# A two-layer convolution block: two ky additions and the last batch norm on VectorE in the tail, a smaller kernel table, and two moves in the first group norm

## The chip, the cores and the metric

The kernel runs on one NeuronCore of one Trainium2 chip (trn2), in fp32. The metric is device microseconds of one execution. The engines are TensorE (PE, with its weight loads PEld), VectorE (DVE), ScalarE (ACT), GpSimd (POOL) and the queue engine SyncE (SP). DMAs are issued from the queues of SP, ScalarE and GpSimd.

## The reference

The input x is 32 images of 128 channels and 32x32 points. Two layers follow each other, each with a residual.

```python
# layer 0: h = group norm (32 groups) of x, as 1024 points of 128 channels
h = einsum('bdl,de->ble', u, W_enc) + b_enc            # 1024 channels
dtA = A * exp(log_dt)[:, None]; Bd = (exp(dtA) - 1) / A
K = 2 * einsum('dn,dnl->dl', Cc * Bd, exp(dtA[:, :, None] * t)).real   # t = 0..63, n = 0..3
y = gelu(causal_convolution(h, K) + D * h)
g = y @ W_glu + b_glu;  g = g[..., :1024] * sigmoid(g[..., 1024:])
x = x + layernorm(h + g) @ W_dec + b_dec
# layer 1: group norm, then a deformable depthwise 8x8 convolution:
# every one of 64 taps samples the image bilinearly at its own offset
acc = sum over taps of w_tap * bilinear(x, position + tap + offset)
x = x + gelu((acc - bn_mean) * bn_inv + bn_beta)
```

## The kernel before

**Table.** `ssm_kernel_table` computes K for all 1024 channels: 8 groups of 128 partitions with 4 terms n, so tiles of 128 partitions by 32 (channel group, n) pairs, and with the 64 steps t tiles of 128x2048. `sincos` reduces an angle (lines 68 to 73), takes two sines on ScalarE and squares the half-angle one. The result `kp` is stored to `kp_d` (line 159). The pool of the table is released afterwards, and the memory is used again by the tiles `z` of the next stage.

**Convolution stage.** `ssm_convolution` runs over 8 blocks k of 128 channels: `encode(k)` makes z, `convolve(k)` multiplies it with Toeplitz tables `toe` read from `kp_d`. Blocks 1 to 7 load u from `u_d`. Block 0 computes u, the group-normed image, on the way, in a loop over t that holds three images at different steps; every engine works through its queue in exactly the written order (`manual_schedule`). `group_norm_steps` yields five steps: the sum (ScalarE, line 169), a matmul (172), the negative mean and the square (ScalarE, 174 and 175), a matmul (178), and root, reciprocal and u (180 to 182). In the loop, image t-2 takes its last step and its u is stored to `u_d` (line 267); image t-1 takes the mean and the square; image t is loaded (272) and takes the sum; `image(t - 3)` multiplies the image that is three back with W_enc (line 237, eight matmuls in two groups g, fp32 matmuls appearing as two instructions each) and adds the bias into z (line 242); then the two matmuls of group norm for t-1 and t follow. u has five buffers, x six.

**Main block.** `main_block` runs two streams of work side by side, each a generator that yields estimated costs; `run_along` always advances the one whose progress is behind. The first stream, `first_parts`, is GLU, layer norm and decode (lines 815 to 875) of images 1 to 31. The second, `second_parts`, is the deformable convolution of all images: per image 17 packs of columns. For a pack, `ds` (hat weights in x, DMA line 1118) is multiplied by `dhy` (hat weights in y, DMA line 1133, shaped on ScalarE at 1153 and 1154) on VectorE at line 1159, TensorE multiplies the windows `dxw` with it (line 1235), and VectorE scales the result by the tap weights into `prod` (line 1251). `prod` has a section for every one of the eight ky. GpSimd adds the eight sections in seven additions, each in two halves (line 1278, 14 instructions), and adds the sum to `dacc` (1286). `prod` has two buffers, `ds` two, `dhy` three half-packs. On SP, the load of `dhy` for a later pack is written behind the multiply that frees its buffer, and the load of `ds` behind that. After an image GpSimd applies the batch norm (line 1297), ScalarE the gelu (1301), VectorE adds x (1302), and ScalarE's queue stores the result (1303). A second stream's step list (`prepare`) puts group norm, offsets (947), the relayout of offsets by DMA (991, 1006), the hat tables (1017 to 1019) and windows (1053) of the next image between the packs.

The first stream ends before the second; the remaining packs of the second run without it.

Of the kernel before, what the change touches and what calls it, by code (L numbers as in the profile page):

```python
# [8 lines left out]
F32 = mybir.dt.float32  # L9
AF = mybir.ActivationFunctionType  # L10
ALU = mybir.AluOpType
# [4 lines left out]
P = 128  # L16
B, C, H, W = 32, 128, 32, 32
# [4 lines left out]
NT = 64  # L22
# [19 lines left out]
def ssm_kernel_table(nc, tc, ins, kp_d):  # L42

    KN = KD * N2
    with tc.tile_pool(name="ssm", bufs=1) as sp:
# [6 lines left out]
        def small(tag, shape=(P, KN)):  # L52
            return sp.tile(list(shape), F32, tag=tag, name=tag)
# [7 lines left out]
        tt = sp.tile([P, NT], F32, tag="tt", name="tt")  # L61
        nc.sync.dma_start(tt, ins["steps"].to_broadcast([P, NT]))

        def sincos(theta, shape, tag):

            k = small(f"{tag}_k", shape)
            r = small(f"{tag}_r", shape)
            nc.vector.tensor_scalar(k, theta, INV_2PI, MAGIC, op0=ALU.mult, op1=ALU.add)
            nc.vector.tensor_scalar(k, k, MAGIC, None, op0=ALU.subtract)
            nc.vector.scalar_tensor_tensor(r, k, -PI2_A, theta, op0=ALU.mult, op1=ALU.add)  # L70
            nc.vector.scalar_tensor_tensor(r, k, -PI2_B, r, op0=ALU.mult, op1=ALU.add)
            nc.vector.scalar_tensor_tensor(r, k, -PI2_C, r, op0=ALU.mult, op1=ALU.add)
            nc.vector.tensor_scalar(r, r, PI_MAX, -PI_MAX, op0=ALU.min, op1=ALU.max)
            s = small(f"{tag}_s", shape)
            nc.scalar.activation(s, r, AF.Sin)
            nc.scalar.activation(k, r, AF.Sin, scale=0.5)
            nc.vector.scalar_tensor_tensor(r, k, -2.0, k, op0=ALU.mult, op1=ALU.mult)
            return s, r
# [45 lines left out]
        cbr, cbi = small("cbr"), small("cbi")  # L124
# [7 lines left out]
        nc.vector.tensor_scalar_mul(cbi, cbi, 2.0)  # L132


        big = (P, KN, NT)
        e, ang = small("e", big), small("ang", big)
        t_b = tt[:, None, :].to_broadcast([P, KN, NT])

        def over_t(a):
            return a[:, :, None].to_broadcast([P, KN, NT])  # L140

        nc.vector.tensor_mul(e, over_t(re), t_b)
        nc.scalar.activation(e, e, AF.Exp)
        nc.vector.tensor_mul(ang, over_t(im), t_b)
        sv, cv = sincos(ang, big, "v")
        nc.vector.scalar_tensor_tensor(cv, cv, 1.0, over_t(cbr), op0=ALU.add, op1=ALU.mult)
        nc.vector.tensor_mul(sv, sv, over_t(cbi))
        nc.vector.tensor_sub(cv, cv, sv)
        nc.vector.tensor_mul(cv, cv, e)

        kp = sp.tile([P, KD, KPW], F32, tag="kp", name="kp")
        nc.gpsimd.memset(kp, 0.0)
# [33 lines left out]
def ssm_convolution(nc, tc, const, ins, x, u_d, kp_d, y_d):  # L186
# [12 lines left out]
    with tc.tile_pool(name="cvt", bufs=3) as tp, tc.tile_pool(  # L199
        name="cvz", bufs=1  # L200
    ) as zp, tc.tile_pool(name="cv1", bufs=1) as one, tc.tile_pool(
        name="cvu", bufs=5
    ) as up, tc.tile_pool(name="cvy", bufs=6) as yp, tc.tile_pool(
        name="cvg", bufs=4
    ) as gp, tc.tile_pool(name="cv_ps", bufs=4, space=PSUM) as psum:

        def banks(name):
            return psum.tile([P, 2, 512], F32, tag="ps", name=name)
# [11 lines left out]
        def block(g, j):  # L220

            return 2 * ORDER[j] + g

        def encode(k):

            z = [
                pool.tile([P, P // 2, NB, B, 2], F32, tag=f"z{g}", name=f"z_{k}_{g}")
                for g, pool in enumerate((one, zp))
            ]
            bias = b_enc[:, k * P : (k + 1) * P]  # L230

            def image(b, u):
                both = banks(f"psz_{k}_{b}").rearrange("p g (j d) -> p g j d", j=NB)
                for g in range(2):
                    for j in range(NB):
                        lo = block(g, j) * P
                        nc.tensor.matmul(  # L237
                            both[:, g, j, :], u[:, lo : lo + P], w_enc[:, k * P : (k + 1) * P],
                            start=True, stop=True,
                        )  # L240
                for g in range(2):
                    nc.vector.tensor_add(  # L242
                        z[g][:, :, :, b, :].rearrange("p d j e -> p j d e"),
                        both[:, g].rearrange("p j (d e) -> p j d e", e=2),
                        bias.rearrange("p (d e) -> p d e", e=2)[:, None].to_broadcast(
                            [P, NB, P // 2, 2]
                        ),
                    )

            if k > 0:  # L250
                for b in range(B):
                    u = up.tile([P, L], F32, tag="u", name=f"u_{k}_{b}")
                    nc.sync.dma_start(u, u_d[b])
                    image(b, u)
                return z


            running = {}

            def step(b):  # L260
                if b in running:
                    next(running[b][1])

            for t in range(B + 3):
                step(t - 2)
                if t - 2 in running:
                    nc.scalar.dma_start(u_d[t - 2], running[t - 2][0])
                step(t - 1)
                if t < B:
                    u = up.tile([P, L], F32, tag="u", name=f"u_{k}_{t}")  # L270
                    xt = yp.tile([P, L], F32, tag="yo", name=f"xt_{t}")
                    nc.sync.dma_start(xt, x[t])

                    def pm(n, t=t):
                        return banks(f"gn_ps_{t}_{n}")[:, 0, 0:1]

                    running[t] = u, group_norm_steps(
                        nc, gp, pm, const["gavg"], const["eps"], xt, u
                    )
                    step(t)  # L280
                if t >= 3:
                    image(t - 3, running.pop(t - 3)[0])
                step(t - 1)
                step(t)
            return z

# [82 lines left out]
        with tc.manual_schedule():  # L369
            for k in range(KD):  # L370
                convolve(k, encode(k))
# [218 lines left out]
def main_block(nc, tc, const, ins, x, u_d, y_d, x1_d, out, offmax):  # L590
# [22 lines left out]
    with ctx:  # L613
# [78 lines left out]
        for i in range(2):  # L692
            t = dram1.tile([2, NCOL], F32, tag=f"rel_d{i}", name=f"rel_d{i}")
            rel_d.append(t)
            t = dram1.tile([P, 2 * ASTEP // P], F32, tag=f"rel_n{i}", name=f"rel_n{i}")
            n = 2 * ASTEP // P
            for lo in range(0, n, HSUB):
                w = min(HSUB, n - lo)
# [381 lines left out]
        packs = [(b, us) for b in range(B) for _, us in PACKS]  # L1080
# [98 lines left out]
        def second_part(b, steps):  # L1179
# [6 lines left out]
            for n in range(NP):  # L1186
# [6 lines left out]
                h = b * NP + n  # L1193
                s = s_of.pop(h)

                for i in range(0, PIECES, 2):
# [10 lines left out]
                    for piece in (i, i + 1):  # L1207
# [7 lines left out]
                        for parts in zip(blocks_of(0, piece), blocks_of(1, piece)):  # L1215
                            rows, run = parts[0][0][1], parts[0][0][3]
                            hi = lo + rows * run * m
                            to = [
                                t[:, lo:hi].rearrange("p (s k v) -> p s k v", s=m, k=rows)
                                for t in ps  # L1220
                            ]
                            for part in range(len(parts[0][1])):
                                for side in range(2):
                                    (ky, _, v0, _, step, skew), wins = parts[side]
                                    w, r0, r1 = wins[part]
                                    half = slice(64 * side, 64 * side + 64)
                                    frm = s[half, 0, ky * NV + v0 - VBASE[side] + r0 :]
                                    frm = bass.AP(
                                        tensor=frm.tensor, offset=frm.offset,
                                        ap=[  # L1230
                                            frm.ap[0], [CELLS, m],
                                            [step * NV + skew, rows], [1, r1 - r0],
                                        ],
                                    )
# [38 lines left out]
                def row(ky, lo=0, hi=m):  # L1273
                    return prod[:, ky * KS + lo * H : ky * KS + hi * H]

                for to, frm in ((2, 0), (3, 1), (4, 6), (5, 7), (2, 4), (3, 5), (2, 3)):
                    for lo, hi in ((0, m // 2), (m // 2, m)):
                        nc.gpsimd.tensor_add(  # L1278
                            row(to, lo, hi), row(to, lo, hi), row(frm, lo, hi)
                        )  # L1280
                total = row(2)
                slot = 0
                for u in us:
                    j0, nj = span_of(u)
                    to = acc[:, u - 7 + j0 : u - 7 + j0 + nj]
# [8 lines left out]
            o = two.tile([P, L], F32, tag="img", name=f"do_{b}")  # L1294
            xr = two.tile([P, L], F32, tag="img", name=f"dxr_{b}")
            nc.sync.dma_start(xr, x1_d[b])
            nc.gpsimd.tensor_scalar(
                o.rearrange("p (h w) -> p w h", w=W), acc, bn_mean, bn_inv,
                op0=ALU.subtract, op1=ALU.mult,
            )  # L1300
# [1 line left out]
            ending.append((11, lambda: nc.vector.tensor_add(o, o, xr)))  # L1302
            ending.append((14, lambda: nc.scalar.dma_start(out[b], o)))

        ending = []
        def measure(slots):

            return slots * 8.0 + 40.0
# [22 lines left out]
        def first_parts():  # L1331

            for b in range(1, B):
                for cost in first_part(b, last=(b == B - 1)):
                    yield cost / FIRST

        def second_parts():

            for cost in opening():
                yield AHEAD * cost / 82.0  # L1340
            for b in range(B):
                steps = prepare(b + 1) if b + 1 < B else []
                for cost in second_part(b, steps):
                    yield cost / SECOND

        run_along((first_parts(), 1.0), (second_parts(), 1.0))
        for _, step in ending:
            step()
# [145 lines left out]
```

## Time and profile before

| | |
|---|---|
| time, median of 3 | 12572.89 us (12570.41 to 12574.23) |
| the profiled execution | 12590.62 us, of it 12588.9 span |
| mean granted TensorE clock | 0.979 |
| PE busy | 12115.7 us (96%) |
| DVE busy | 7661.0 us (61%) |
| ACT busy | 5537.8 us (44%) |
| POOL busy | 8789.7 us (70%) |
| first `psy` matmul of the convolution of block 0 | 181.25 us |
| last matmul of the GLU stream (gpv) | 12116.5 us |
| last batch norm on GpSimd | 12572.49 to 12577.13 us |

Times inside the profile are counted from the start of the span. A row of the timeline gives start and duration, engine, line and operation, output and inputs, shape and count; in brackets stands the idle time of the engine before it and what ended it. A row of the table of waits gives who waited for whom, the total in us, how often, and the longest. The chain of waits is followed back from the last instruction to whatever released it at each step.

### The profile page before, as it was taken

What the parts mean: (1) busy time and instruction counts of PE and PEld (TensorE: products, weight loads), DVE (VectorE), ACT (ScalarE), POOL (GpSimd) and SP (SyncE); (2) the same over time, 40 slices, a digit from 0 to 9 for tenths busy, and PEclk for the clock granted to TensorE, in tenths of its full rate; (3) what the DMA queues carried; (4) which work ended last, traced back from release to release, by engine and by line L of the source; (5) the groups of instructions that cost most, each with busy time, mean ns of one, the idle gap of its engine ahead of it and who ended that gap; (6) DMA issues with size and microseconds to landing.
All of it is one profiled execution on the core that took longest, in us unless ns stands there. A gap on an engine that the chain in (4) does not pass through costs nothing.

```text
span 12588.9 us, 161534 instructions
## 1 busy us (share of the span) xinstructions
PE 12115.7 (96%) x51362; PEld 6608.0 (52%) x51362; DVE 7661.0 (61%) x14315; ACT 5537.8 (44%) x7852; POOL 8789.7 (70%) x11691
## 2 busy tenths in 40 slices
PE   7999889999999999999999999999999999999975
PEld 7999444444444444444444444444444444444443
DVE  5555136666666666666666666666666666666666
ACT  4344124444444444444444444444444444444444
POOL 2455227777777777777777777777777777777778
PEclk9999999999999999999999999999999999999986
DMA  7899236766666666666666666666667667666666
GB/s 236 267 276 277 83 98 185 187 184 184 180 183 180 185 178 182 186 184 181 188 184 187 184 180 185 179 187 180 179 187 186 180 186 186 186 185 184 183 176 177
DMA packets 1521947, 2350.43 MB, mean 187 GB/s; under 512 B 619586, under 2 KB 835266, under 8 KB 1520066
## 3 DMA queue, kind: packets, MB, share of 16 engines
q1 hardware_dynamic: 1382210, 2027.97, 60.1%
q10 hardware_dynamic: 89728, 177.76, 4.2%
q0 software_dynamic: 49152, 134.28, 3.6%
q8 instruction: 414, 6.78, 0.2%
q14 instruction: 443, 3.63, 0.1%
HBM read 2016.61 MB, written 407.02 MB: 193 GB/s over the span
## 4 chain that ended last, share of the span: by engine, by line
PE 77%; DMA 10%; ACT 5%; DVE 3%; issue 2%; SPq 2%; POOL 1%; ACTq 0%; DVEq 0%; POOLq 0%
PE gpv L838 24%; PE gpg L815 23%; PE dps L1235 15%; DMA dhat<-dh 5%; PE psy L320 5%; PE psz L237 3%; PE gpo L743 3%; PE gph L854 3%; DMA rel_d<-rel_n 1%; ACT dh L1018 1%; ACT dh L1017 1%; ACT dhy L1153 1%; POOL prod L1278 1%; DVE ds L1159 1%; DMA dr<-rel_d 1%
## 5 line engine op out<-in xcount | busy, mean ns | idle before, releaser
L1278 POOL TENSOR_TENSOR prod<-prod 128x256 f32<-128x256 f32 (+3 forms) x7616 | 5531.4, 767 | 1211.5 <-DVE prod L1251 1211.5
L1251 DVE TENSOR_TENSOR prod<-dps,k_weight_slots 128x512 f32<-128x512 f32 (+16 forms) x8704 | 3127.5, 407 | 1948.0 <-PE dps L1235 1743.5
L815 PE MATMUL gpg<-gy,g_w_glu 128*128 128x512 f32 x8192 | 3741.9, 600 | 14.3 <-DMA gy<-y_d 14.3
L838 PE MATMUL gpv<-gy,g_w_glu 128*128 128x512 f32 x8192 | 3732.1, 599 | 0.0
L1235 PE MATMUL dps<-ds,dxw 64*128 64x128 f32 (+14 forms) x23936 | 2700.2, 371 | 235.4 <-DVE prod L1251 171.5
L1159 DVE TENSOR_TENSOR ds<-ds,dhy 128x640 f32<-128x640 f32 (+2 forms) x2176 | 2260.0, 1075 | 929.0 <-ACT dhy L1154 673.3
L1235 PEld LDWEIGHTS dps<-ds,dxw 64*128 64x128 f32 x23936 | 1924.2, 194 | 1287.3 <-issue 480.6
L815 PEld LDWEIGHTS gpg<-gy,g_w_glu 128*128 128x128 f32 x8192 | 1511.2, 190 | 1926.2 <-issue 1862.1
L838 PEld LDWEIGHTS gpv<-gy,g_w_glu 128*128 128x128 f32 x8192 | 1514.6, 190 | 1909.2 <-issue 1909.2
L739 POOL TENSOR_TENSOR gs<-gs,gq 128x256 f32<-128x256 f32 x896 | 865.7, 987 | 1820.8 <-ACT gq L875 1820.8
L1153 ACT ACTIVATE dhy<-dhy,k_minus_y 128x640 f32<-128x640 f32 (+2 forms) x2176 | 1697.8, 780 | 384.2 <-DMA dhy<-rel_d 138.1
L1154 ACT ACTIVATE dhy<-dhy,one 128x640 f32<-128x640 f32 (+2 forms) x2176 | 1725.8, 793 | 71.2
L875 ACT ACTIVATE gq<-gr 128x512 f32<-128x512 f32 x448 | 282.3, 630 | 2793.1 <-DVE gr L867 2775.9
L822 ACT ACTIVATE gs<-gpg,k_b_glu 128x512 f32<-128x512 f32 x512 | 350.8, 685 | 1657.0 <-PE gpg L815 1655.7
L357 POOL DMA_DIRECT2D y_d<-yo x1024 | 591.5, 585 | 692.2 <-ACT yo L344 634.1
L846 DVE SCALAR_TENSOR_TENSOR gs<-gpv,k_b_glu,gs 128x512 f32<-128x512 f32 x512 | 382.9, 748 | 1008.6 <-PE gpv L838 983.2
L1286 POOL TENSOR_TENSOR dacc<-dacc,prod 128x256 f32<-128x256 f32 (+6 forms) x1184 | 862.8, 729 | 55.2
L739 POOL TENSOR_TENSOR gs<-gs,gr 128x256 f32<-128x256 f32 x896 | 798.0, 911 | 0.0
L320 PE MATMUL psy<-toe,z 128*128 128x192 f32 x4096 | 668.3, 326 | 7.6 <-DVE z L242 5.5
L320 PEld LDWEIGHTS psy<-toe,z 128*128 128x128 f32 x4096 | 663.4, 196 | 11.7 <-DVE z L242 6.8
L854 PE MATMUL gph<-gu,k_W_enc 128*128 128x512 f32 x1024 | 529.2, 598 | 27.7 <-DVE gs L846 27.4
L335 DVE TENSOR_TENSOR psy<-psy,t 128x256 f32<-128x256 f32 (+2 forms) x768 | 333.8, 435 | 346.3 <-ACT t L328 329.5
(164 smaller groups left out, 6020.0 us busy)
## 6 DMA issues: line engine op xcount, KB each, us to landing
dhy<-rel_d SPq DMA_DIRECT2D x3264, 160.0 KB
ds<-dhat SPq DMA_DIRECT2D x832, 400.0 KB
ds<-dhat SPq DMA_DIRECT2D x448, 480.0 KB
dxw<-dxw_d SPq DMA_DIRECT2D x832, 224.0 KB
y_d<-yo POOLq DMA_DIRECT2D x1024, 128.0 KB, 4.2
gy<-y_d SPq DMA_DIRECT2D x512, 256.0 KB
u<-u_d SPq DMA_DIRECT2D x224, 512.0 KB
dhat<-dh ACTq DMA_DIRECT2D x256, 390.0 KB
```

The source lines that it names most:

```text
L320: nc.tensor.matmul(ps[:, c // 2, c % 2, :], rows[i][:, (g * CG + c0 + c) // 2, c % 2, :], toe[:, c0 + c, :], start=True, stop=True,)
L739: nc.gpsimd.tensor_add(to[:, cut], to[:, cut], more[:, cut])
L815: nc.tensor.matmul(gate, w_glu[:, k, D + m * P : D + m * P + P], ys[k], start=(k == 0), stop=(k == KD - 1),)
L838: nc.tensor.matmul(val, w_glu[:, k, m * P : m * P + P], ys[k], start=(k == 0), stop=(k == KD - 1),)
L854: nc.tensor.matmul(h, w_enc[:, m * P : (m + 1) * P], u, start=True, stop=True)
L1153: nc.scalar.activation(t, t, AF.Abs, bias=minus_y)
L1154: nc.scalar.activation(t, t, AF.Relu, scale=-1.0, bias=const["one"])
L1159: nc.vector.tensor_mul(s_of[h][:, cut], s_of[h][:, cut], t)
L1235: nc.tensor.matmul(to[side][:, :, :, r0:r1], xw[half, w, :], frm, start=True, stop=True,)
L1251: nc.vector.tensor_mul(bass.AP(tensor=at_y.tensor, offset=at_y.offset, ap=[at_y.ap[0], [H, m], [step * (KS - 1) + skew, rows], [1, run],], ...
L1278: nc.gpsimd.tensor_add(row(to, lo, hi), row(to, lo, hi), row(frm, lo, hi))
L1286: nc.gpsimd.tensor_add(to, to, total[:, slot * H : (slot + nj) * H].rearrange("p (s y) -> p s y", y=H),)
```

## The change

It has four parts. The kernel table evaluates exponentials, sines and cosines only at 16 of the steps: the eight multiples (written 8a + 7 in the reversed order of the steps) and the last eight, and forms the 64 by complex products of the two, so that most tiles have 128x512 elements. In block 0, the store of u is issued from GpSimd's queue instead of ScalarE's, and the second group norm matmul of image t-1 stands between the two halves of the matmuls of image t-3 instead of behind them. In the packs that come after the first stream has ended, VectorE makes the additions of ky 0 into 2 and 1 into 3, each as one instruction, and in the very last pack those of 6 into 4 and 7 into 5 as well. The batch norm of the last image runs on VectorE.

```diff
-        big = (P, KN, NT)
-        e, ang = small("e", big), small("ang", big)
+        few = (P, KN, 16)
+        t16 = sp.tile([P, 16], F32, tag="t16", name="t16")
+        nc.vector.tensor_copy(t16[:, 0:8], tt[:, 7::8])
+        nc.vector.tensor_copy(t16[:, 8:16], tt[:, NT - 8 : NT])
+        e, ang = small("e", few), small("ang", few)
...
-        nc.vector.scalar_tensor_tensor(cv, cv, 1.0, over_t(cbr), op0=ALU.add, op1=ALU.mult)
-        nc.vector.tensor_mul(sv, sv, over_t(cbi))
-        nc.vector.tensor_sub(cv, cv, sv)
-        nc.vector.tensor_mul(cv, cv, e)
+        nc.vector.scalar_tensor_tensor(cv, cv, 1.0, e, op0=ALU.add, op1=ALU.mult)
+        nc.vector.tensor_mul(sv, sv, e)
+        w = [small(f"w{i}", (P, KN, 8)) for i in range(3)]
+        near = cv[:, :, 8:], sv[:, :, 8:]
+        nc.vector.tensor_mul(w[0], near[0], over_t(cbr, 8))
+        nc.vector.tensor_mul(w[2], near[1], over_t(cbi, 8))
+        nc.vector.tensor_sub(w[0], w[0], w[2])
+        nc.vector.tensor_mul(w[1], near[0], over_t(cbi, 8))
+        nc.vector.tensor_mul(w[2], near[1], over_t(cbr, 8))
+        nc.vector.tensor_add(w[1], w[1], w[2])
+        parts = []
+        for i, far in enumerate((cv, sv)):
+            o = small(f"o{i}", (P, KN, 8, 8))
+            nc.vector.tensor_mul(
+                o,
+                w[i][:, :, None, :].to_broadcast([P, KN, 8, 8]),
+                far[:, :, :8, None].to_broadcast([P, KN, 8, 8]),
+            )
+            parts.append(o.rearrange("p n a b -> p n (a b)"))
+        cv = parts[0]
+        nc.vector.tensor_sub(cv, cv, parts[1])
...
-            def image(b, u):
+            def image(b, u, between=None):
...
+                    if g == 0 and between is not None:
+                        between()
...
-                    nc.scalar.dma_start(u_d[t - 2], running[t - 2][0])
+                    nc.gpsimd.dma_start(u_d[t - 2], running[t - 2][0])
...
                 if t >= 3:
-                    image(t - 3, running.pop(t - 3)[0])
-                step(t - 1)
+                    image(t - 3, running.pop(t - 3)[0], between=lambda: step(t - 1))
+                else:
+                    step(t - 1)
...
                 for to, frm in ((2, 0), (3, 1), (4, 6), (5, 7), (2, 4), (3, 5), (2, 3)):
+                    if alone and frm in ((0, 1, 6, 7) if h + 1 == len(packs) else (0, 1)):
+                        nc.vector.tensor_add(row(to), row(to), row(frm))
+                        continue
...
-            nc.gpsimd.tensor_scalar(
+            finish = nc.vector if b == B - 1 else nc.gpsimd
+            finish.tensor_scalar(
...
-        ending = []
+        ending, alone = [], []
...
+            alone.append(True)   # at the end of first_parts
```

More of the change, by code (lines that the diff above doesn't have):

```diff
@@ L132, in ssm_kernel_table, with over_t @@
         nc.vector.tensor_scalar_mul(cbi, cbi, 2.0)
-        big = (P, KN, NT)
-        e, ang = small("e", big), small("ang", big)
-        t_b = tt[:, None, :].to_broadcast([P, KN, NT])
-        def over_t(a):
-            return a[:, :, None].to_broadcast([P, KN, NT])
+        few = (P, KN, 16)
[3 more added lines that the diff above has]
+        e, ang = small("e", few), small("ang", few)
+        t_b = t16[:, None, :].to_broadcast([P, KN, 16])
+        def over_t(a, n=16):
+            return a[:, :, None].to_broadcast([P, KN, n])
         nc.vector.tensor_mul(e, over_t(re), t_b)
@@ L144, in ssm_kernel_table @@
         nc.vector.tensor_mul(ang, over_t(im), t_b)
-        sv, cv = sincos(ang, big, "v")
-        nc.vector.scalar_tensor_tensor(cv, cv, 1.0, over_t(cbr), op0=ALU.add, op1=ALU.mult)
-        nc.vector.tensor_mul(sv, sv, over_t(cbi))
-        nc.vector.tensor_sub(cv, cv, sv)
-        nc.vector.tensor_mul(cv, cv, e)
+        sv, cv = sincos(ang, few, "v")
+        nc.vector.scalar_tensor_tensor(cv, cv, 1.0, e, op0=ALU.add, op1=ALU.mult)
[19 more added lines that the diff above has]
+        nc.vector.tensor_sub(cv, cv, parts[1])
         kp = sp.tile([P, KD, KPW], F32, tag="kp", name="kp")
```

## The prediction

> **What bounds the kernel now.** I read the slices of the page first. TensorE is 96% busy, and at full clock from about 200 us to 12130 us; the change touches nothing that runs there. What is left is two ends: the first 180 us (table, and group norm with encode of block 0) and the last 450 us, where the GLU matmuls have run out.
>
> ```profile
> PE   7999889999999999999999999999999999999975
> PEclk9999999999999999999999999999999999999986
> ```
>
> *The start: the timeline, then the table of waits for 50 to 185 us.* Columns: start, duration, engine, line, operation, and in brackets the idle time before it and what ended it.
>
> ```profile
> 42.05 0.39 SPq L159 DMA_DIRECT2D kp_d<-kp  x1
> 47.25 0.69 DVE L242 TENSOR_TENSOR z<-psz,b_enc 128x512 f32<-128x512 f32 x1 [5.27 <-DMA kp_d<-kp]
> ...
> 61.55 0.81 DVE L182 TENSOR_SCALAR u<-xt,gn_m,gn_r 128x1024 f32<-128x1024 f32 x1
> 62.40 0.34 ACTq L267 DMA_DIRECT2D u_d<-u  x1
> 62.79 0.17 ACT L174 ACTIVATE gn_m<-gn_ps 128x1 f32<-128x1 f32 x1 [1.47 <-DVE u L182]
> ```
> ```profile
> DVE z L242 <- PE psz L237: 47.7, 24, 3.1
> ACT gn_m L174 <- DVE u L182: 34.4, 22, 2.3
> ```
>
> To see: VectorE is held by the table until 42 us; the add into z then waits for the table's store, which still holds z's memory. After that every image has ScalarE stand still because the store of u, issued from its queue, waits for VectorE's u; gn_m of the next image is behind it. From the u at 48.05 to that of image 31 at 177.5 there are 29 steps, 4.46 us each (mostly 4.1, every third 5.3).
>
> *Why some take 5.3: the one-microsecond windows* (PE, PEld, DVE, ACT, POOL busy, granted clock, DMA share, GB/s).
>
> ```profile
> 107.00:108.00 1.00, 0.00 (x0) 0.00 (x0) 1.00 (x2) 0.70 (x2) 0.00 (x0) 1.00 0.28 74
> 109.00:110.00 1.00, 0.34 (x4) 0.26 (x3) 0.07 (x1) 0.90 (x3) 0.00 (x0) 1.00 1.00 377
> 112.00:113.00 1.00, 0.83 (x5) 0.54 (x3) 0.27 (x1) 1.00 (x3) 0.00 (x0) 0.50 0.97 209
> ```
>
> Clock 0.50 comes back for about 6.8 us of every 13.5 us, after some 3.5 us in which TensorE was about half busy. The 16 matmuls of an image then take 3.75 instead of 2.03 us.
>
> *The end: the chain of waits* (start, duration, what).
>
> ```profile
> 12498.43 8.91 DMA ds<-dhat
> 12507.43 0.06 DVE ds L1159
> ...
> 12512.90 12.01 POOL prod L1278 x14
> ...
> 12526.42 11.44 POOL prod L1278 x14
> ...
> 12539.34 11.57 POOL prod L1278 x14
> ...
> 12572.49 4.65 POOL do L1297
> 12577.16 1.16 ACT do L1301
> ```
> ```profile
> SPq L1133 <- DVE ds L1159: 73.3, 20, 10.0
> ```
>
> To see: from 12346 to 12509 a loop of loads sets the pace, some 14 us a pack: last weight multiply (L1159), SP issues dhy (L1133, which waits for it), then ds, the transfer of some 8 us, next multiply. GpSimd only binds from 12512.9 on, five packs, and in short pieces at 12137-12179 and 12328-12346.
>
> **The change part by part.**
>
> *Table.* Before, VectorE has ten two-input operations at 128x2048 (e, ang, three reductions of the angle, the square of the half angle, four combinations) at 2.29 us, and three TENSOR_SCALARs at 1.22: 26.5 us. After: e, ang, three reductions, square, cv and sv are 8 at 128x512 (0.69, rows L155-157) = 5.5; three TENSOR_SCALARs, between 0.17 (128x32) and 1.22, by line 0.42 each = 1.3; two copies 0.3; six products at 128x256, between 0.19 and 0.69, 0.42 each = 2.5; two 128x2048 products and the difference 6.9. Sum 16.5, so 10.0 less. ScalarE's three 1.9 us functions become about 0.63 (row L875). VectorE had hardly a gap here; shorter work shows waits for ScalarE's sines behind the image's own operations and table loads. I keep 8 of the 10 (ends: 5 and 11). The kp_d store (5.1) and the z add behind it move with it.
>
> *Store of u from GpSimd's queue.* 32 issues of 0.35 leave ScalarE, 32 of 0.585 (row L357, the same kind of store) go to GpSimd, which is 0.00 busy from 48 to 180; behind them in its queue are only the y stores from 191.9. The wait for u goes with the issue. What is late next: gn_m needs the mean's matmul (L172). Let T be the end of that matmul. ScalarE: gn_m to the square's end 1.50, to the identity's end 2.54. TensorE, with the square's matmul (L178) put between the two halves of the image: first half T to T+1.0, L178 waits to T+1.53, second half from T+1.77 to 2.79, L172 ends at T+3.17. So 3.2 us a step at full clock. This new wait of L178 holds the second half, L172 and the z adds; without it the step would be 2.95, so `between` by itself costs 0.2 here and gives an earlier root for the next u. VectorE (0.15 + 0.81 + 1.29) and the 16 DMA engines (share 0.64 x 4.46 = 2.9 a step) lie below. With DMA this near I take 3.5: 29 x (4.46 - 3.5) = 27.8 us. At half clock TensorE alone needs about 4.7.
>
> Here a rule is weighed. The row: the clock fell at 111 us after 3.5 us of half-busy TensorE with no gap over 2.2 us. The Trainium skill, "TensorE: Matmul & The Clock Gate" (What's actually happening), has it fall only after an idle window of about 3.4 us. By the rule the step would stay warm: 27.8. If, against it, windows as full as the new ones (2.8 of 3.5 us) still let it fall half of the time, the mean step is 13.5 / (6.75/4.7 + 6.75/3.5) = 4.0 and the gain 13. The trace contradicts the rule's letter, but the windows before a fall were 47-50% busy and the new ones would be 80%: I take warm.
>
> *Additions to VectorE.* The flag is set when the first stream is used up. By the yielded costs (31.051 images against 30.691 + 0.357 at the end of pack 5) that is pack 6 of image 30: 28 packs. Each loses 4 of 14 half additions on GpSimd (0.875 mean in the tail: 3.5 us) and adds two 128x512 ones on VectorE: 0.69 alone, about 1.1 beside GpSimd (L1159, 128x640, takes 0.82 alone and up to 1.34). I take 0.9: 1.8 a pack. Queued behind them: the next pack's scaling, then the weight multiplies, dhy and ds. Of the 1.8, 0.74 falls into the wait that VectorE has there for TensorE; the other 1.1 into its waits for ds, 1.3 to 3.4 a pack in the load loop. Cover is lacking at the pack from 12430 and among the offset taps at 12180-12235: cost 2. If none of it were covered: 23 packs x 1.1 = 25.
>
> The second rule, which speaks against the change: "GPSIMD Engine Reference" (Key points) says that VectorE instructions with two SBUF inputs contend with GpSimd, and these have two. The rows agree in kind (L1278 128x256 has 0.69 undisturbed, 0.875 mean). By the row GpSimd keeps 3.5 - 0.5 = 3.0 a pack; if it stood still for the whole 2.2, 1.3. Either matters only where GpSimd binds.
>
> Where it binds: 12137-12179: pack 5 is unchanged, and VectorE's next scaling waited only 1.16 us for GpSimd: 0.5. 12328-12346, last pack of image 30: 2.5. The last five packs, worked forward from the scaling that ends at 12512.8: VectorE adds to 12514.6, scales to 12518.1, multiplies (ds lands at 12520.1) to 12522.0, scales to 12525.1, adds to 12526.9, scales to 12530.3, multiplies to 12534.0, scales to 12537.1, adds to 12538.9, scales to 12542.1, multiplies to 12546.5, scales to 12549.1, adds to 12550.6, scales the last pack to 12556.7. GpSimd's ten additions (8.5 + 1.5) follow within each gap, so VectorE now binds. The last pack's four additions at 0.6 end at 12559.1, GpSimd's six halves (0.62 each) at 12562.3 after the third, its four sums (1.9) at 12564.3. Before: 12572.5. So 8.2.
>
> *Last batch norm.* 4.65 on GpSimd becomes a 128x1024 TENSOR_SCALAR with a transposed write: between 0.81 (L182) and 2.14 (L964, a transposed write beside GpSimd); GpSimd is done by then, so 1.2. Gain 3.4; nothing hides it.
>
> Tail: 0.5 + 2.5 + 8.2 + 3.4 - 2 = 12.6.
>
> **Sum.** 8 + 27.8 + 12.6 = 48.4 us. The profiled execution took 12590.6 (span 12588.9 and 1.7 around it), 17.7 above the median 12572.9; the savings lie in stretches that repeat, so I take them off the median: 12524.5.
>
> **The rivals.**
> *The clock keeps falling in block 0:* for it, it fell at 68% mean duty; against, the fuller windows. 8 + 13 + 12.6 = 34: 12539. Chance 0.20.
> *The step does not shorten, or the tail's cover is thin:* DMA or the earlier waits hold 4.46, 8 + 12.6 = 21, 12552; or 23 uncovered packs take 25 from 48, 12550. Chance 0.20.
> *The store of u lands late (slower than before):* u has five buffers, so the store of image t must land before image t+5's first pass, three steps later. L357's 128 KB stores land after 4.2 (up to 8.8); this one has 512 KB. Landing in L makes the step L/3: at 15.5 us the step is 5.2 and the gain of table and tail is gone; at 19 it is 6.3, and 29 x 1.87 - 21 = 33 slower: 12606. Against it: stores and loads of 512 KB each already pass every 4.46 us. Chance 0.06.
> My forecast: 0.54.
>
> **How the numbers follow.** What a measurement here can tell from no change is 0.2%, 25 us. The forecast with its bounds (3.2 to 3.8 a step, table 5 to 11, tail 6 to 17) spans 12503 to 12541. The range reaches to the second rival: 12503 to 12556. Faster: forecast 0.54, first rival 0.18 of its 0.20, a third of the second, 0.06: 0.78. Same: 0.16. Slower: 0.06.
>
> **What would show it.** kp_d issued near 32-34 us; no wait "gn_m <- u"; steps of u of 3.2 to 3.8 us; clock near 1.0 from 50 us to the end of encode; TensorE's psy starting near 145 us. In the tail load-bound packs still some 14 us, POOL prod x10 at 8 to 9 us, VectorE without gaps from 12514 to 12557 (less the shift), and about 12 us less from the last ds transfer to the end. A clock of 0.5 in block 0, a step over 4.2, or packs lengthened by 1 us and more in the load loop would prove it wrong.

## The result, and the profile after

The changed kernel took 12518.77 us (median of 6 runs, 12512.21 to 12530.76) beside 12573.11 for the kernel before (6 runs, 12562.27 to 12580.32): 54.3 us less, ratio 0.9956 (95% interval 0.9946 to 0.9966). Predicted were 12524.5, with a range of 12503 to 12556, and 48.4 less. The total holds, but its terms don't: the first group norm gave more than was said, the tail less, and the two errors partly cancel.

Lines of the changed kernel have moved: the group norm matmuls 172 and 178 are 192 and 198, gn_m 174 is 194, u 182 is 202, the z add 242 is 264, the store of u 267 is 289; in the tail the weight multiply 1159 is 1182, the scaling 1251 is 1274, the additions on GpSimd 1278 are 1304 and those on VectorE 1301. The rows of every other run carry the line numbers of its own kernel.

The slices of the page:

```profile
PE   8999989999999999999999999999999999999975
PEclk9999999999999999999999999999999999999985
```

The two ends are still where the time is. At the start, the timeline (start, duration, engine, line, operation; in brackets the idle time before and what ended it):

```profile
31.47 0.39 SPq L179 DMA_DIRECT2D kp_d<-kp  x1
...
38.09 0.69 DVE L264 TENSOR_TENSOR z<-psz,b_enc 128x512 f32<-128x512 f32 x1 [6.71 <-DMA kp_d<-kp]
...
88.19 0.81 DVE L202 TENSOR_SCALAR u<-xt,gn_m,gn_r 128x1024 f32<-128x1024 f32 x1
...
88.41 0.38 PE L198 MATMUL gn_ps<-gn_ss,gavg 128*128 128x1 f32 x2 [0.53 <-ACT u L195]
...
89.29 0.53 POOL L289 DMA_DIRECT2D u_d<-u  x1 [2.50 <-DVE u L202]
...
89.94 0.17 ACT L194 ACTIVATE gn_m<-gn_ps 128x1 f32<-128x1 f32 x1 [0.40 <-PE gn_ps L192]
...
91.22 0.81 DVE L202 TENSOR_SCALAR u<-xt,gn_m,gn_r 128x1024 f32<-128x1024 f32 x1
```

The table's store is issued 10.6 us earlier (42.05 before). From u to u it is 3.03 us. The wait for u stands in front of GpSimd's store (2.50 us, and nobody is behind it), and gn_m waits only 0.40, for its own mean. The table of waits for 50 to 150 us says it in sums: the 34.4 us that gn_m spent behind u (50 to 185 us of before) are gone, and 10.1 for the mean's matmul have come.

```profile
POOL u_d L289 <- DVE u L202: 67.8, 27, 2.9
...
PE gn_ps L198 <- ACT u L195: 13.4, 25, 0.5
...
ACT gn_m L194 <- PE gn_ps L192: 10.1, 25, 0.4
```

From the u at 38.89 to that of image 31 at 127.62 there are 29 steps, 3.06 us each in the mean; the first `psy` matmul comes at 131.54 and not at 181.25.

At the end, the chain of waits no more goes through 12 us of GpSimd a pack. Up to 12478 it goes through the loads of ds, which land just as VectorE comes to them (from 12445.9 to 12492.4 VectorE waits for 0.7 us in all), and from there through VectorE:

```profile
12473.10 4.96 DMA ds<-dhat
...
12478.41 3.70 DVE ds L1182 x3
...
12492.35 2.02 DVE prod L1301 x3
...
12494.44 4.03 POOL prod L1304 x6
...
12500.37 1.17 DVE do L1324
12501.56 1.16 ACT do L1328
```

Between the two ends, from the first `psy` to the batch norm of image 30, before's trace takes 12160 us and after's 12142. Nothing in it is changed but a few packs at its end. The kernels below took 12141 to 12152 there on two chips, 12160 to 12170 on a third and 12217 on a fourth, with no order by the part of the change that they have. So this stretch goes by chip and execution, and the 18 us are not counted as the change's; before's profiled execution was 17.7 above its median, and the prediction had taken the savings off the median for that reason.

### The profile page after: what moved, and what is told of

Read it like the earlier page. It is cut to its first block, busy times and chain, and to the rows that moved or that the text cites. A ratio compares the mean times of both kernels' runs of the same rounds, so it can differ in the third digit from the quotient of the medians.

```text
span 12512.1 us, 161570 instructions
## 1 busy us (share of the span) xinstructions
PE 12107.6 (97%) x51362; PEld 6597.6 (53%) x51362; DVE 7718.5 (62%) x14383; ACT 5532.7 (44%) x7851; POOL 8734.0 (70%) x11606
## 4 chain that ended last, share of the span: by engine, by line
PE 78%; DMA 10%; ACT 5%; DVE 3%; issue 2%; SPq 1%; POOL 0%; ACTq 0%; DVEq 0%; POOLq 0%
PE gpv L861 24%; PE gpg L838 23%; PE dps L1258 15%; DMA dhat<-dh 6%; PE psy L343 5%; PE psz L257 3%; PE gpo L766 3%; PE gph L877 3%; DMA rel_d<-rel_n 1%; ACT dh L1041 1%; ACT dh L1040 1%; DMA ds<-dhat 1%; ACT dhy L1176 1%; DVE ds L1182 1%; DVE prod L1274 1%
## 5 line engine op out<-in xcount | busy, mean ns | idle before, releaser
L1304 POOL TENSOR_TENSOR prod<-prod 128x256 f32<-128x256 f32 (+3 forms) x7500 | 5450.7, 766 | 1276.3 <-DVE prod L1274 1274.6
```

The costliest lines, as they stand in the source:

```text
L1304: nc.gpsimd.tensor_add(row(to, lo, hi), row(to, lo, hi), row(frm, lo, hi))
```

## The experiments

Each group of runs has its own runs of the kernel before on the same chip; differences are against those. Before took 12578.4 us beside e1 to e4, 12578.9 beside e5 to e8, 12597.7 beside e9 to e11 and 12645.6 beside e12, so medians of different groups are not compared with each other. Three numbers are read from each profile: the first `psy` matmul, the mean step (from the third u of block 0 to the last, over 29), and the tail, split at GpSimd's first addition of the sixth pack of image 30, at the batch norm of that image, at GpSimd's first addition of the fifth pack from the end and at the last add of x.

| kernel | median, us | against before | ratio, 95% interval | step | first psy |
|---|---|---|---|---|---|
| before (first profile) | 12573.11 | | | 4.46 | 181.25 |
| after | 12518.77 | -54.3 | 0.9946 to 0.9966 | 3.06 | 131.54 |
| e1 table alone | 12567.00 | -11.4 | 0.9986 to 1.0003 | 4.45 | 170.12 |
| e2 store alone | 12535.65 | -42.7 | 0.9956 to 0.9980 | 2.93 | 137.31 |
| e3 matmul between the halves alone | 12640.27 | +61.9 | 1.0042 to 1.0069 | 6.57 | 242.20 |
| e4 tail alone | 12570.67 | -7.7 | 0.9987 to 1.0004 | 4.46 | 181.15 |
| e5 after without the matmul between | 12518.01 | -60.9 | 0.9939 to 0.9966 | 2.93 | 128.19 |
| e6 after once more, beside e5 | 12525.00 | -53.9 | 0.9945 to 0.9972 | 3.06 | 131.71 |
| e7 before, 6 matmuls added twice an image | 12589.51 | +10.6 | 1.0002 to 1.0018 | 4.93 | 194.85 |
| e8 after, half of the stores of u | 12530.62 | -48.3 | 0.9949 to 0.9976 | 3.05 | 131.56 |
| e9 before, 2 matmuls added twice an image | 12584.73 | -13.0 | 0.9985 to 0.9998 | 4.13 | 171.91 |
| e10 after, additions in the last five packs only | 12536.43 | -61.3 | 0.9939 to 0.9966 | 3.05 | 131.53 |
| e11 e5 and e10, one addition a pack | 12535.91 | -61.8 | 0.9941 to 0.9969 | 2.95 | 128.62 |
| e12 e3 with late z adds | 12636.59 | -9.0 | 0.9982 to 1.0000 | 4.17 | 168.15 |

**e1, the table alone.** The edit is the table's part of the diff, nothing else.

> Only the kernel table is changed, all else as before. Theory: the first u after the table comes 9 us earlier (48.05 becomes about 39), the loop over the images of block 0 keeps its mean step of 4.46 us, and the whole is 8 to 9 us faster: about 12564. Rival, the 17 us that the middle lost between the two traces belong to the change and to this part: then about 12547. Rival, the start does not bind: no difference.

11.4 us faster by the medians, with an interval that reaches no change; the profile is sharper: third u at 37.15 and not 48.05, first `psy` 11.1 earlier, step unchanged. The theory holds, with 11 for its 8 to 9. The rival, 17 more us from the middle, falls: it had the median at about 12547. So does the other, that the start does not bind, by the first `psy`.

**e2, the store of u alone.**

```diff
-                    nc.scalar.dma_start(u_d[t - 2], running[t - 2][0])
+                    nc.gpsimd.dma_start(u_d[t - 2], running[t - 2][0])
```

> Only the store of u goes from ScalarE's queue to GpSimd's, without the square's matmul between the two halves of an image. Theory: the wait for u leaves ScalarE, TensorE is busy enough that its clock stays at 1.0, and the step falls from 4.46 to 3.0: 29 x 1.45 = 42 less, 12531. Rival A, the clock still falls for half of the time: step 4.0, 12560. Rival B, the root comes too late without the matmul between the halves and the step stays above 3.5: 12545 or more.

42.7 us faster, first `psy` 43.9 earlier. Its timeline, from u to u:

```profile
86.08 0.81 DVE L182 TENSOR_SCALAR u<-xt,gn_m,gn_r 128x1024 f32<-128x1024 f32 x1
...
88.70 0.17 ACT L174 ACTIVATE gn_m<-gn_ps 128x1 f32<-128x1 f32 x1 [0.33 <-PE gn_ps L172]
...
89.03 0.81 DVE L182 TENSOR_SCALAR u<-xt,gn_m,gn_r 128x1024 f32<-128x1024 f32 x1
```

2.95 us, the number that the prediction worked out for a step without the matmul between the halves. This one line of the diff is most of the change, and both rivals fall: the clock is 1.00 in every 15 us window from 60 to 225 us, and the root is not late.

**e3, the matmul between the halves alone.**

```diff
+                    if g == 0 and between is not None:
+                        between()
...
-                    image(t - 3, running.pop(t - 3)[0])
-                step(t - 1)
+                    image(t - 3, running.pop(t - 3)[0], between=lambda: step(t - 1))
+                else:
+                    step(t - 1)
```

> Only the square's matmul is put between the two halves of an image; the store of u stays in ScalarE's queue. Theory: ScalarE's wait for u ends the step as before, so 4.46 stays or changes by less than 0.15: 12573 within 4. Rival: the root comes earlier by the time of eight matmuls, and the wait for u is shorter by as much: 0.5 to 1.0 a step, 15 to 29 us faster, 12544 to 12558.

Neither: 61.9 us slower. The waits for 50 to 230 us (who waited for whom: total, times, longest):

```profile
DVE z L244 <- PE psz L237: 117.6, 27, 4.5
ACT gn_m L174 <- DVE u L182: 106.2, 27, 4.0
PEld gn_ps L178 <- ACT u L175: 68.5, 28, 5.2
PE gn_ps L178 <- ACT u L175: 60.6, 28, 4.9
```

Three engines wait for one another in a ring. ScalarE can't start gn_m until its queue has issued the store of u; u stands behind the z adds on VectorE; the z adds need the second half of the image on TensorE; that half now stands behind the square's matmul, which needs gn_m. One turn takes 6.57 us in the mean.

A part of that is the clock. TensorE now stands still for 2.0 to 2.4 us in every turn, and its clock is at 0.50 for most of the loop. The window of 105 to 120 us (PE, PEld, DVE, ACT, POOL busy, granted clock, DMA share, GB/s), then the eight matmuls of half an image in e3 and in after:

```profile
105.00:120.00 15.00, 10.93 (x49) 10.35 (x48) 5.97 (x12) 5.20 (x12) 0.00 (x0) 0.50 0.40 140
```
```profile
122.35 0.58 PE L178 MATMUL gn_ps<-gn_ss,gavg 128*128 128x1 f32 x2 [2.03 <-ACT u L175]
122.80 2.05 PE L237 MATMUL psz<-w_enc,u 128*128 128x128 f32 x8
```
```profile
100.78 1.14 PE L257 MATMUL psz<-w_enc,u 128*128 128x128 f32 x8
```

At clock 0.50 a step takes 6.66; the one from 94.0 to 99.6 us, where the clock was back for about 3.4 us, took 5.62. The steps of before take 4.10 at full clock, as those of e9 below. So of the 2.11 us a step that e3 lost against before, some 1.5 are the ring's and some 0.6 the lower clock; this is an estimate from these steps, and no run separates the two.

**e12, the ring opened at one place.** e3 with the two z adds of an image issued after the next u instead of ahead of it:

```diff
+                if between is None:
+                    add(0), add(1)
+                else:
+                    late.extend((lambda: add(0), lambda: add(1)))
...
                 step(t - 2)
+                while late:
+                    late.pop(0)()
```

> The kernel before with the edit to image() alone (the store of u stays in ScalarE's queue), and the two z adds of an image issued after the next u on VectorE instead of ahead of it. Theory: with the edit alone the step is 6.57 because a ring is closed: ScalarE's gn_m waits for u, u stands behind the z adds on VectorE, these wait for the second half of the image on TensorE, which stands behind the square's matmul, and that needs gn_m. With the adds behind u the ring is open: from gn_m to the root's end 2.6, reciprocal, u and the store's issue 1.7, so a step of 4.3 to 4.5 and about the time of before (within 10). Rival: the matmuls' order alone makes the step, then it stays above 6 and the kernel is 45 to 65 slower than before.

A step of 4.17 and 9.0 us faster than before by the medians, with an interval that reaches no change, and the same matmul order as e3. The wait of the z adds for TensorE all but ends (50 to 150 us):

```profile
ACT gn_m L174 <- PE psz L237: 20.6, 14, 1.5
...
ACT gn_m L174 <- DVE u L182: 7.4, 5, 1.5
DVE z L244 <- PE psz L237: 1.5, 4, 0.4
```

What is left is the wait of before: gn_m starts only behind the issue of u's store. (In many steps the table puts this wait, of the same 1.47 us, down to a matmul that ended later than u.)

```profile
90.08 0.35 ACTq L277 DMA_DIRECT2D u_d<-u  x1
...
90.47 0.17 ACT L174 ACTIVATE gn_m<-gn_ps 128x1 f32<-128x1 f32 x1 [1.47 <-DVE u L182]
```

So the matmuls' order alone is not the cause of e3's loss; the ring is, together with the clock that its waits let fall (from 60 to 160 us the clock is 0.83 in e12). Of the 13.1 us by which the first `psy` is earlier than before, 5.8 come from the third u (42.29), which no longer stands behind the z adds that wait for the table's store.

**e5 and e6, after without the matmul between the halves, and after beside it.**

```diff
...
-                    image(t - 3, running.pop(t - 3)[0], between=lambda: step(t - 1))
-                else:
-                    step(t - 1)
+                    image(t - 3, running.pop(t - 3)[0])
+                step(t - 1)
```

> The changed kernel with the square's matmul back ahead of the image, so without the edit to image(). Theory: as in the run that moved the store alone, the step is 2.95 instead of 3.03, so 29 x 0.08 = 2 us faster than the changed kernel: about 54 to 62 below before, and the first psy matmul 2 to 4 us earlier than 131.5. Rival: the edit is what keeps the step short once the table is early, then the step rises above 3.2 and the kernel is 5 or more slower than the changed one.

> The changed kernel unchanged, on the same chip as the one without the edit to image(). Theory: ratio 0.9956 again, about 55 below before; from the first psy matmul to the end some 12381 us, as the kernel with the tail alone had (12383), because the 17 us that the middle seemed to lose belong to the one profiled execution of before. Rival, that the middle really gains by the change: 12381 here too, but then the profile of the warm clock run, which has neither table nor tail, should show 12407 and not 12390 for that stretch.

Once the store is out of ScalarE's queue, the edit costs 0.13 us a step, 3.5 at the first `psy`. By the medians it is 7.0, the runs of the two (12511.4 to 12522.9 and 12523.1 to 12525.9) touching but not overlapping; their intervals against before overlap, so only the profile's 3.5 is clear. The edit is not what keeps the step short. From the first `psy` to the end e6 took 12390 us, where the theory had 12381 as in after's trace, and e7 12394, where the rival had 12407: the middle does not gain by the change.

**e7 and e9, the clock by itself.** The store stays in ScalarE's queue, and TensorE is given matmuls whose results are not used, ahead of each of the two group norm matmuls (6 in e7, 2 in e9):

```diff
-                        return banks(f"gn_ps_{t}_{n}")[:, 0, 0:1]
+                        ps = banks(f"gn_ps_{t}_{n}")
+                        for i in range(6):
+                            nc.tensor.matmul(
+                                ps[:, 1, 0:P], const["gavg"], w_enc[:, 0:P],
+                                start=True, stop=True,
+                            )
+                        return ps[:, 0, 0:1]
```

> The kernel before with six more 128x128 matmuls ahead of each of the two group norm matmuls of an image; their results are not used. The store of u stays in ScalarE's queue. Theory: TensorE is then busy some 3.5 of every 4.1 us and its clock stays at 1.0; the steps of 5.3 vanish and the mean goes from 4.46 to 4.1: 29 x 0.36 = 10 less, 12563 to 12568. So of the 43 us of the store a quarter would be the clock and the rest ScalarE's wait. Rival: the clock falls all the same, and the extra matmuls take 1.5 at full clock and 3 at half: step above 5, 15 or more slower.

Six were too many: each is two instructions, 1.50 us a group and not the 0.75 that I reckoned. TensorE is busy for 15.00 of 15.00 us and makes a step of 4.93. It says only that the clock stays up then.

> The kernel before with two more matmuls ahead of each group norm matmul instead of six (1.0 us an image instead of 3.0); the store of u stays in ScalarE's queue. Theory: TensorE is busy some 3.6 of every 4.1 us, the clock stays at 1.0 and no step takes 5.3: mean step 4.1, 29 x 0.36 = 10 less than before, 12568. Then of the 43 us of the store some 10 are the clock and some 33 ScalarE's wait. Rival: the clock does not matter, the step stays at 4.4 to 4.5, 12579. Rival, the clock still falls: above 4.7, 12586 or more.

With two, the windows of 90 to 105 us (PE, PEld, DVE, ACT, POOL busy, granted clock, DMA share, GB/s), first before, then e9:

```profile
90.00:105.00 15.00, 12.08 (x72) 11.34 (x72) 6.97 (x13) 9.43 (x23) 0.00 (x0) 0.75 0.73 258
```
```profile
90.00:105.00 15.00, 13.66 (x106) 12.33 (x106) 8.19 (x15) 8.99 (x21) 0.00 (x0) 1.00 0.79 252
```

The clock is 1.00 from 60 us on, from 57 us on no step takes over 4.4, and the mean step is 4.13: 13.0 us by the medians, 29 x 0.33 = 9.6 by the profile. ScalarE's wait is untouched and sets that step:

```profile
95.64 0.17 ACT L174 ACTIVATE gn_m<-gn_ps 128x1 f32<-128x1 f32 x1 [1.47 <-DVE u L182]
```

So of e2's gain some 10 us are the clock, which stays up there without added matmuls, and 29 x (4.13 - 2.93) = 35 are the wait.

**e8, are the DMA engines the bound?** After, with

```diff
-                if t - 2 in running:
+                if t - 2 in running and t % 2:
...
```

This leaves out the store of u for every even image. Later readers load the odd image's u in its place, so that they read as many bytes; the output is not that of the block.

> The changed kernel with the store of u left out for every even image (later readers take the odd image's u instead, so that as many bytes are read). Theory: the engines' own chain makes the step, 3.03, and it stays there although the DMA share falls from 1.0 to about 0.75. Rival, the DMA engines at share 1.0 bind: a quarter of the bytes less makes the step 2.3 to 2.7, 10 to 20 us faster than the changed kernel.

The step is 3.05. The same windows, after and e8:

```profile
90.00:105.00 15.00, 12.32 (x101) 11.37 (x100) 10.68 (x21) 12.94 (x30) 2.67 (x5) 1.00 1.00 343
```
```profile
90.00:105.00 15.00, 12.32 (x101) 11.37 (x100) 10.69 (x20) 12.96 (x30) 1.58 (x3) 1.00 0.74 272
```

In this window a fifth fewer bytes move, the DMA share falls to 0.74, and no engine's busy time changes but GpSimd's, which issues fewer stores: a share of 1.00 was not a bound. The medians agree: e8 is not faster than e6 (12530.6 and 12525.0), where the rival had 10 to 20 us less.

**e4, the tail alone.** The last hunks of the diff (additions and batch norm).

> Only the tail is changed: two additions over ky on VectorE (four in the last pack) and the last batch norm on VectorE. Theory: the last five packs are 9.9 us shorter as in the trace of after, nothing before them moves by more than 1: 12563. Rival, the additions also take time in the middle or in the load loop that only shows in a median: 12566 to 12573. Rival, the middle gains 17 us from this part: 12546.

7.7 us, with an interval that reaches no change. The stretches of the tail, from seven profiles with the tail of before (before, e1, e2, e3, e7, e9, e12) and five with that of after (after, e4, e5, e6, e8):

| stretch | as before, mean | as after, mean | e10 | e11 |
|---|---|---|---|---|
| sixth pack to batch norm of image 30 | 203.8 (202.7 to 205.3) | 203.6 (202.5 to 204.3) | 202.7 | 203.8 |
| to the fifth pack from the end | 169.7 (167.0 to 171.6) | 172.3 (171.8 to 172.8) | 171.8 | 169.6 |
| to the add of x | 65.6 (65.3 to 66.4) | 56.9 (56.1 to 57.5) | 56.1 | 56.4 |

The last five packs give 8.7 us, where the theory had 9.9; the load loop before them is 2.6 longer in the mean, where it had no more than 1; the packs of image 30 give nothing. The net is 6.3. The 2.6 are not shown to be the additions': e10 below makes none in the load loop and took 171.8 there, and two of the seven with the tail of before, e3 and e12, are low by themselves (167.0 and 167.9).

**e10, the additions in the last five packs only.**

```diff
-                    if alone and frm in ((0, 1, 6, 7) if h + 1 == len(packs) else (0, 1)):
+                    if alone and b == B - 1 and h + 5 >= len(packs) and frm in ((0, 1, 6, 7) if h + 1 == len(packs) else (0, 1)):
```

> The changed kernel with the two additions on VectorE in the last five packs only; the 23 packs before them add on GpSimd as in the kernel before. Theory: in the load loop the additions cost 1 us in all (from the batch norm of image 30 to the fifth pack from the end 172.3 becomes 171.3), in the last packs of image 30 nothing is lost: 0 to 1 us faster than the changed kernel, too little for the medians. Rival, the prediction's own: cost 2 there, gain 3 in the packs where GpSimd binds, so 1 slower. Rival, the 23 packs carry part of the tail's gain: 4 or more slower.

The last five packs are the same 56.1, and the other two stretches together are 374.5, against 375.9 with the additions in all packs and 373.5 with none. The rival that the other 23 packs carry part of the tail's gain falls. What their additions cost is 2.4 by the means of after and before and 1.4 against e10, one profile; both lie inside the spread of single profiles, so theory and the prediction's own cost of 2 are not told apart. The medians don't tell either: 61.3 below before, with an interval that overlaps that of after.

**e11, one addition instead of two.** e5 and e10 together, with `(0,)` in place of `(0, 1)`.

> The changed kernel without the edit to image(), with one addition (not two) on VectorE in the packs before the last, four in the last, and this in the last five packs only. Theory: VectorE binds in those packs of the changed kernel with some 1.5 us of idle GpSimd in each; one addition less on VectorE is 0.9 less a pack there, and two halves more on GpSimd 1.8 more, so the two are level: 0 to 3 us less in the last five packs (56.8 becomes 54 to 57), with 2 to 3 from the step and 1 from the load loop: 12515 to 12520 where before is 12578. Rival: GpSimd binds again and the last five packs are 2 to 5 us longer, 12520 to 12526.

The last five packs take 56.4: inside the theory's 54 to 57, and so no case of the rival, but no less than e10's 56.1 with two additions. GpSimd's additions now come almost back to back, while VectorE waits for transfers of ds (12463 to 12521 us):

```profile
DVE ds L1179 <- DMA ds<-dhat: 2.8, 4, 1.6
POOL prod L1301 <- DVE prod L1271: 2.7, 2, 1.7
```

GpSimd, VectorE and the loads of ds are level here, and taking one addition back gains nothing. By its ratio (0.9955) e11 is no different from after (0.9956) or e5 (0.9952); none of the variants is shown to beat the changed kernel by what the medians can tell, though a step of 2.93 speaks for leaving the edit to `image()` out.

## Why the prediction was right, and which terms were not

That the total came within 6 us is partly luck. The mechanism of the main parts was right, but the first group norm gave 12.7 us more than its term and the tail 6.3 less. Of the signs that the prediction names, kp's store (31.5 us, for 32 to 34), the step (3.06, for 3.2 to 3.8) and the first `psy` (131.5, for 145) all came earlier or shorter than said. Its bounds, summed again from their parts, give 12508 to 12543 and not 12503 to 12541; the measured time lies in both.

**Table: 8 predicted, 9.2 measured (10.9 when alone).** The ten us less of VectorE's work did arrive: kp is stored 10.6 earlier. The two us that I kept back for waits on ScalarE's sines were not needed: up to the store of kp the table of waits of after has no wait of VectorE for ScalarE. What came off in after is the store, 6.6 us from its issue to the z add instead of 5.2.

**Store and matmul order: 27.8 predicted, 40.5 measured** (from the third u to the first `psy`: 133.2 before, 92.65 after). The chain was right: I worked out 3.17 with the matmul between the halves and 2.95 without; the traces show 3.03 and 2.95. What was mis-sized is the step after it, "With DMA this near I take 3.5". The 16 DMA engines do stand at share 1.00 now, but e8 shows that they don't bind a step of 3.05. 29 x (3.5 - 3.06) = 12.8 is the whole error of this term. That the edit to `image()` costs a little was right in sign (0.2 predicted, 0.13 measured); that without the moved store it would cost 62 us I had not seen, nor did my expectation for e3.

**The clock.** I took warm, against the row that had fallen at gaps under 2.2 us, because the windows would be fuller; at 12.3 of 15 us busy it did stay at 1.00. The Trainium skill's rule ("TensorE: Matmul & The Clock Gate", What's actually happening: a fall only after an idle window) gave the same answer here, so after does not choose between them; the trace of before remains against its letter, and e3 more so: there the clock is 0.50 from 105 to 150 us with no gap of TensorE over 2.1.

**Tail: 12.6 predicted, 6.3 by the stretches, 7.7 by the median of e4.**
- The last batch norm: 3.4 predicted; GpSimd's 4.65 became VectorE's 1.16, 3.5.
- The last five packs: 8.2 predicted beside it, 8.7 - 3.5 = 5.2 measured. The additions cost 0.9 each as assumed and VectorE is gapless as said, with the loads of ds level with it; the mis-sized term is the weight multiplies, "multiplies (ds lands at 12520.1) to 12522.0" and "multiplies to 12534.0". From the first scaling to the end of the last I had 43.9 us; the trace has 46.4 (12445.94 to 12492.35). The groups of the last five packs (count, busy us, mean ns), before and then after:

```profile
L1278 POOL TENSOR_TENSOR prod<-prod 128x256 f32<-128x256 f32 x42 | 35.1, 878 | 1.7 <-DVE prod L1251 1.7
...
L1159 DVE TENSOR_TENSOR ds<-ds,dhy 128x640 f32<-128x640 f32 x7 | 8.0, 1155 | 1.3 <-DMA dxw<-dxw_d 1.0 <-issue 0.3
```
```profile
L1304 POOL TENSOR_TENSOR prod<-prod 128x256 f32<-128x256 f32 x30 | 27.9, 968 | 6.7 <-DVE prod L1274 6.7
...
L1182 DVE TENSOR_TENSOR ds<-ds,dhy 128x640 f32<-128x640 f32 x7 | 9.2, 1337 | 0.7 <-issue 0.7
...
L1301 DVE TENSOR_TENSOR prod<-prod 128x512 f32<-128x512 f32 x6 | 5.5, 955 | 0.1
```

  With VectorE busy almost without a gap, a GpSimd addition takes 90 ns more in the mean and a multiply 182. This is how contention would look, and the prediction had weighed it for the additions alone; no run here isolates it as the cause.
- 12137 to 12179 and the last pack of image 30: 0.5 + 2.5 predicted, 0.2 measured. In after that last pack is 1.8 us shorter from GpSimd's first addition to the batch norm (12.48 to 10.71), but the packs ahead of it are 1.2 longer (191.3 to 192.5).
- The uncovered additions: 2 predicted, 2.6 by the means, and not shown to be theirs (e10).

Terms that were too small by 1 and 13 and one that was too large by 5 to 6 add up to 8; the medians differ by 6 from the forecast. The rivals: the clock did not fall, the step did shorten, and the store of u, though each of its transfers shares full queues, was never late: it landed 6.2 us after its issue in the median and 7.1 at most, where the rival needed over 15, and no engine waited for it in block 0.

## What to carry to other kernels

A DMA issue in the queue of a computing engine carries its wait with it: look at what stands behind it in that queue, and give the issue to an engine with nothing behind. A reordering that looks free must be followed round through every in-order queue, since two harmless orders (a store ahead of gn_m, a matmul ahead of half an image) close a ring together that neither closes alone. A DMA share near 1.0 need not be a bound; work out the engines' own chain and take the chain, unless a run with fewer bytes moves the step.

## What the runs showed of the hardware

- The DMA engines show a share of 1.00 at 343 GB/s and of 0.74 at 272 GB/s with the same step. Before showed 0.73 at 258 GB/s, so the share roughly follows the bytes moved, yet full is not late: in the table of waits of after, 50 to 150 us, no engine waits for a load of x.
- TensorE's clock fell with windows of 12.1 of 15 us busy at half clock for part of the time (before), and stayed up with 12.3 of 15 at full clock (after), with gaps of 0.5 us. In e3 it stayed at 0.50 from 105 to 150 us, with 10.9 of 15 us busy at half clock and gaps of 2.0 us. No run here settles at what busy share it falls.
- With VectorE and GpSimd both nearly gapless in the last five packs, both were slower: a 128x640 multiply of two SBUF inputs on VectorE took 1.34 us in the mean where it had taken 1.16, and GpSimd's 128x256 additions 0.97 where they had taken 0.88.
